# First-group tables in two pairs: into-state tables turned unscaled, scales put into the out-of-state tables

## The chip, the cores and the metric

The kernel runs on one core of a Trainium2 chip. The metric is the device time of one execution in microseconds (us); lower is better. The engines spoken of are TensorE (PE in the profile; PEld is its weight load), Vector (DVE), ScalarE (ACT), GpSimd (POOL) and Sync (SP, which here only issues DMAs). A name with q (SPq) is an engine's queue of DMA issues.

## The reference

For 64 batches, 64 heads and 1024 positions, x passes through a state-space convolution and then a gated low-rank feed-forward layer, and is added to the result:

```python
# per head h: 64 complex states n
dtA = (-exp(log_A_real) + 1j*A_imag) * exp(log_dt)[:, None]
Cs  = (C[...,0] + 1j*C[...,1]) * (exp(dtA) - 1.0) / A
K   = 2.0 * einsum('hn,hnl->hl', Cs, exp(dtA * l)).real      # length 1024
u_m = x * mask                                               # l < length[b]
y   = (causal convolution of u_m with K + u_m * D) * mask
# tokens are rows of y of 1024 features
scores = y @ Wr.T                        # 64 experts
gates  = softmax of the 16 largest scores
h   = einsum('nd,krd->nkr', y, A)        # 64 experts of rank 16
out = x + 2.0 * einsum('nkr,kdr->nd', h * gates, B)
```

All is float32.

## The kernel before

The 1024 positions of a head are cut into 8 chunks of 128. Within a chunk the convolution is a 128x128 Toeplitz matrix; between chunks it goes through the 64 complex states. So each head needs four kinds of table, made from its parameters: the *into-state* table (turned, so that it can be the stationary operand of the matmul that takes a chunk into the states; tile `bt`), the *out-of-state* table (tile `w`), the factor by which a state goes on over one chunk (tile `turn`), and the Toeplitz matrix (tile `toep`). The tables are values of exp(dtA l) at l of the constant row `lv`: magnitude exp(re l) from ScalarE (`mag`), sine and 1 - 2 sin^2 of half the angle from ScalarE's Sin (`sn`, `sh`), the angle reduced to one turn by Vector. Before the change the into-state table carries the scale of C: `alpha`, `nbeta`, `nalpha` are columns with one value for each state of a head, computed by a chain of small Vector operations from the parameters (`exp_parts`, `real_part`, `angle`, `products`).

Heads go in 8 groups of 8 (`HG`); a group has 4 pairs of heads (`GP`), and one tile holds a pair, 64 states of each head on 128 partitions. Group g runs as `conv(g)`: `into_states` (the `pu` matmuls, L742, copied out by ScalarE, L747) for each pair, `recur` on Vector over the 7 chunks (L786), `inside` (Toeplitz products into `pc` banks, L828 and L836), `across` (states out through `w`, L851), `evict` (Vector, times the length mask, L862). Then come gates and the feed-forward products (`first`, L687, tile `h`), which use a seven-product scheme for 2x2 blocks. The factors of A for that scheme are sums of its quarters: the first eight are formed on TensorE by identity matmuls (`factors_by_identity`, L211, seen as `sum`, copied out by ScalarE L216 and L220); two more sums are accumulating DMAs that GpSimd issues after the copy `landed` (L224), which waits for the last Toeplitz load.

The first group is special: nothing runs before it. Its tables come from `tables(0)`, stepped by hand. For each pair, Vector scales `w` into `b` (L497, L503), TensorE transposes it (`turned_table`, L440, tile `pb`), ScalarE copies it to `bt` (L442). For each two pairs, `kernels` multiplies the scaled table by the matrix `heads` (L328, `pk`), which adds the states of each head to the row of K; ScalarE copies it (`ks`, L331 to L333), Vector adds D, Sync stores it to `krows` in HBM (L372), and three loads (L356) read it back shifted by one element for each partition, which gives `toep`.

What order things run in:

- While `first_order` is open, Vector runs in the order in which the code names its operations; while `first_copies` is open, so does ScalarE.
- On TensorE, GpSimd and the queues a planner picks the order by estimated readiness and program order, except where `keep_in_program_order` pins an instruction behind the one before it on its engine, and `issue_after` behind a named one.
- `together` takes one step of each of several generators in turn, `some(it, n)` takes n steps.
- `ps_k` has 2 PSUM buffers, for `pb`, `pk` and the first group's `pu`. `ps_f` has 4, for `sum`, for `pc` of pairs 1 and 3 of the first group, and for `h`. `ps_c` has 2, for `pc` of pairs 0 and 2.

Of the kernel before, what the change touches and what calls it, by code (L numbers as in the profile page):

```python
# [44 lines left out]
P = 128  # L45
NB = 64
# [61 lines left out]
def body(ctx: ExitStack, tc, x, xo, lens, par, dvec, dgrp, at, bm, wt, cst, out):  # L108
# [36 lines left out]
    lens_sb = prep.tile([P, NB], I32, tag="lens", name="lens_sb")  # L145

# [14 lines left out]
    def load_x(h):  # L161
        t = xp.tile([P, 2, NBLK * NB], F32, tag="x", name=f"x_{h}")
        marks["x"] = nc.sync.dma_start(t, x[h : h + 2].rearrange("h p c -> p h c"))
        x_tiles[h] = t
# [8 lines left out]
    def quarters(wpool, w, name, queue, fine=False):  # L173
# [16 lines left out]
        for n, i in ((0, 0), (1, 0), (0, 2), (1, 2), (2, 0), (2, 2), (3, 0), (3, 2))[2 * fine :]:  # L190
            load(n, i)
# [51 lines left out]

    wa_quarters = quarters(wp, at, "wa", nc.sync, True)
    load_x(0)
    nc.sync.dma_start(lens_sb, lens.partition_broadcast(P))
    load_x(2)
    load_x(4)
    load_x(6)
# [19 lines left out]
    scales = {}  # L269

    def tables(g):
# [43 lines left out]
        if g == 0:  # L315
            turn, toep = others()
            tabs[g] = (w, bt, turn, toep)
        h0 = g * HG
        if g == 0:
            all_rows = tabp.tile([2, GP, P], F32, tag="mag", name=f"ks_{g}")  # L320

        def kernels(bbs, i):


            n = i + 2 * len(bbs)
            pk = ps_k.tile([2, n - i, P], F32, tag="pk", name=f"pk_{g}_{i}")
            for m, bb in enumerate(bbs):
                nc.tensor.matmul(pk[:, 2 * m : 2 * m + 2, :], lhsT=heads, rhs=bb[:, :, 0, :],  # L328
                                 start=True, stop=True)
            ks = all_rows[:, i:n, :]  # L330
            nc.scalar.copy(ks, pk)  # L331
            nc.scalar.copy(ks[0:1, :, :HP], pk[0:1, :, HP:])
            nc.scalar.copy(ks[0:1, :, HP:], pk[0:1, :, :HP])  # L333
            return ks, i, n
# [14 lines left out]
        def load_toeplitz(i, n):  # L349


            row = krows[h0 + 2 * i : h0 + 2 * i + 1, :]
            heads_of = toep[:, 2 * i : 2 * n, :].rearrange("p (i a) c -> p a i c", a=2)

            def load(o, count, start):
                nc.sync.dma_start(  # L356
                    o, bass.AP(row.tensor, row.offset + start, [[1, count], [2 * KROW, n - i], [1, P]]))

# [85 lines left out]
        for i in range(GP if g < DIRECT else 0):  # L444
# [14 lines left out]
            if g:  # L459
                if i % 2:  # L460
                    yield
# [1050 lines left out]
```

## Time and profile before

| | us |
|---|---|
| median of 3 runs (lowest, highest) | 941.73 (941.72, 941.85) |
| the profiled execution's own time | 941.79 |
| its span, first to last instruction | 940.0 |
| TensorE busy | 929.5 |
| Vector busy | 741.0 |
| GpSimd busy | 337.0 |
| ScalarE busy | 164.1 |

The page of the profile shows busy times and shares of the span, the span in 40 slices, the chain of work that ended last (followed back from the last instruction to what released each step), and groups of instructions by line. A line of a timeline has the start, the duration, the engine, the line, the operation, output and inputs, how many instructions were merged, and in brackets the idle time before and what ended it. A line of the chain has start, duration and what. Times are in us from the start of the span; a mean of one instruction is in ns. A float32 matmul is two passes, and so two instructions; a transpose is one. Buffer numbers are left out of names: `was` and `waa` are quarters and sums of A.

### The profile page before, as it was taken

To read this page: it belongs to the slowest core of one execution; us is meant where nothing else is said; L and a number is where in the kernel's file an instruction comes from. 1 tells how busy PE (TensorE), PEld (TensorE's weight loads), DVE (VectorE), ACT (ScalarE), POOL (GpSimd) and SP (SyncE) were. 2 spreads that over 40 slices of the span, in tenths; PEclk is the share of its full clock that TensorE was granted. 3 is DMA by queue.
4 is the path that set the end of the run, shared out by engine and by line. 5 is a ranking of instruction groups with operands and counts; after the bars stand their busy time and mean duration, and the time that the engine had idled before them with its cause. 6 is when DMAs were issued, how large, how long until landed. Compare 5 with 4: busy or idle time off the path is not lost.

```text
span 940.0 us, 14255 instructions
## 1 busy us (share of the span) xinstructions
PE 929.5 (99%) x5384; PEld 743.2 (79%) x5384; DVE 741.0 (79%) x1725; ACT 164.1 (17%) x314; POOL 337.0 (36%) x284
## 2 busy tenths in 40 slices
PE   7999999999999999999999999999999999999998
PEld 2576768688588588588588788888888888888887
DVE  8899798797996995995892497879856866785674
ACT  5343233411411411510300000000000000000000
POOL 0113213052052052052052032356746555764555
PEclk9999999999999999999999999999999999999999
DMA  8635335347454444444242463754672574358332
GB/s 291 186 87 168 107 110 156 108 126 189 125 144 154 124 138 159 125 128 169 90 131 101 152 246 124 255 203 140 212 275 79 191 270 155 110 205 307 95 123 101
DMA packets 72298, 149.47 MB, mean 159 GB/s; under 512 B 10054, under 2 KB 21030, under 8 KB 72230
## 3 DMA queue, kind: packets, MB, share of 16 engines
q1 hardware_dynamic: 52546, 99.65, 32.1%
q0 software_dynamic: 16864, 47.22, 16.0%
q10 hardware_dynamic: 2820, 1.70, 0.6%
q8 instruction: 42, 0.69, 0.3%
q14 instruction: 26, 0.21, 0.1%
HBM read 100.13 MB, written 47.33 MB: 157 GB/s over the span
## 4 chain that ended last, share of the span: by engine, by line
PE 93%; DVE 6%; issue 0%; DMA 0%; ACT 0%; DVEq 0%
PE h L687 39%; PE s L1272 35%; PE pu L742 5%; PE pc L851 4%; PE psh L947 3%; PE pc L828 3%; PE pc L836 1%; DVE bt L492 1%; DVE hg L492 1%; DVE f L492 1%; DVE f L503 0%; PE psc L959 0%; PE pb L440 0%; PE last L1272 0%; DMA par_sb<-in_par 0%
## 5 line engine op out<-in xcount | busy, mean ns | idle before, releaser
L786 DVE SCALAR_TENSOR_TENSOR s<-s,turn 128x64 f32<-128x64 f32 (+1 forms) x432 | 122.8, 330 | 2.8 <-ACT s L747 2.3
L687 PE MATMUL h<-y,waa 128*128 128x256 f32 x512 | 116.7, 380 | 0.0
L687 PE MATMUL h<-y,was 128*128 128x256 f32 x512 | 116.2, 379 | 0.0
L687 PE MATMUL h<-ty,was 128*128 128x256 f32 x512 | 116.0, 379 | 0.0
L687 PEld LDWEIGHTS h<-y,waa 128*128 128x128 f32 x512 | 96.3, 190 | 15.0 <-issue 1.9
L687 PEld LDWEIGHTS h<-ty,was 128*128 128x128 f32 x512 | 97.1, 190 | 13.9 <-issue 0.8
L687 PEld LDWEIGHTS h<-y,was 128*128 128x128 f32 x512 | 96.8, 190 | 13.7 <-DVE b L503 0.4
L1034 POOL TENSOR_TENSOR hg<-h_p,gx 128x512 f32<-128x512 f32 x16 | 35.6, 2223 | 141.6 <-DVE h_p L503 107.1
L1007 POOL DMA_DIRECT2D gx<-gt_dram x56 | 33.9, 618 | 145.1 <-DMA gt_dram<-gt 145.1
L1286 ACT COPY p<-s 128x512 f32<-128x512 f32 x28 | 16.4, 585 | 312.4 <-PE s L1272 312.4
L1034 POOL TENSOR_TENSOR hg<-h_u,gx 128x512 f32<-128x512 f32 x32 | 45.1, 1409 | 63.8 <-DVE h_u L492 36.6
L1131 POOL TENSOR_TENSOR o<-o,acc_a 128x512 f32<-128x512 f32 x32 | 47.6, 1506 | 41.4 <-ACT acc_a L1149 32.5
L687 PE MATMUL h<-ty,waa 128*128 128x256 f32 x256 | 58.4, 381 | 0.0
L687 PEld LDWEIGHTS h<-ty,waa 128*128 128x128 f32 x256 | 48.2, 190 | 8.3 <-DVE rsn L492 0.8
L742 PE MATMUL pu<-x,bt 128*64 128x448 f32 x256 | 53.0, 546 | 0.4
L862 DVE TENSOR_TENSOR y<-pc,mask 128x512 f32<-128x512 f32 x64 | 40.2, 680 | 16.4 <-PE pc L851 16.4
L1131 POOL TENSOR_TENSOR o<-o,b_room 128x512 f32<-128x512 f32 x32 | 49.1, 1555 | 9.8 <-DVE b_room L492 9.8
L492 DVE TENSOR_TENSOR o<-o,s 128x512 f32<-128x512 f32 x50 | 34.1, 681 | 23.0 <-PE s L1272 17.9
L1037 POOL DMA_DIRECT2D hg_dram<-hg x32 | 25.6, 800 | 67.4 <-DVE hg L492 46.6
L1131 POOL TENSOR_TENSOR o<-o,u 128x512 f32<-128x512 f32 x36 | 45.3, 1282 | 10.0 <-DVE u L492 9.7
L492 DVE TENSOR_TENSOR hg<-hg 128x512 f32<-128x512 f32 x64 | 42.4, 682 | 4.7 <-POOL hg L1034 4.3
L1272 PE MATMUL s<-qy,wbs 128*128 128x256 f32 x192 | 44.1, 379 | 0.0
(275 smaller groups left out, 1678.8 us busy)
## 6 DMA issues: line engine op xcount, KB each, us to landing
x<-in_x SPq DMA_DIRECT2D x32, 512.0 KB
hg_dram<-hg POOLq DMA_DIRECT2D x16, 1024.0 KB, 6.0
o<-in_xo SPq DMA_DIRECT2D x64, 256.0 KB
out<-o SPq DMA_DIRECT2D x63, 256.0 KB
gx<-gt_dram POOLq DMA_DIRECT2D x56, 256.0 KB, 4.8
qy<-hg_dram SPq DMA_DIRECT2D x28, 512.0 KB
r<-hg_dram SPq DMA_DIRECT2D x26, 512.0 KB
hg_dram<-hg POOLq DMA_DIRECT2D x16, 768.0 KB, 4.5
```

Of the source, the lines that this page charges most:

```text
L492: V.tensor_tensor(out=o, in0=a, in1=b, op=o_)
L687: nc.tensor.matmul(bank[:, ii, :], lhsT=fac[n - 1][:, k, (j + ii) * P : (j + ii + 1) * P], rhs=rf[n - 1][:, k, :], start=(first and ii == ...
L742: nc.tensor.matmul(pu[hh * NS : (hh + 1) * NS, :], lhsT=bt[:, i, (1 - c) * P + hh * NS : (1 - c) * P + (hh + 1) * NS], rhs=xt[:, hh, : NCH ...
L786: return V.scalar_tensor_tensor(out=o, in0=a, scalar=scalar, in1=b, op0=op0, op1=op1)
L828: nc.tensor.matmul(pcs[hh][half_of(e, 1), chunks(e)], lhsT=toep[:, 2 * i + hh, HP:], rhs=xt[:, hh, chunks(e)], start=True, stop=False, ski ...
L851: m = nc.tensor.matmul(pcs[hh][half_of(e, late), into], lhsT=w[o : o + NS, c, i, seg : seg + HP], rhs=s[o : o + NS, c, of].rearrange("p k ...
L862: marks["y"] = V.tensor_tensor(out=y[:, :, i // 2, 2 * (i % 2) + hh, :], in0=pcs[hh].rearrange("p (k b) -> p k b", b=NB), in1=mask, op=ALU ...
L947: nc.tensor.matmul(phalf[o : o + NE, :], lhsT=wt_sb[:, d, :], rhs=yf[:, d, :], start=(d < 2), stop=(d >= NBLK - 2),)
L1007: i = queue.dma_start(gx[:, ii, :], gt_dram[g, c * n : (c + 1) * n, :].unsqueeze(1).to_broadcast([n, RANK, TOK]),)
L1034: G.tensor_tensor(out=o, in0=a, in1=b, op=op)
L1131: tc.keep_in_program_order(G.tensor_tensor(out=o, in0=a, in1=b, op=op_))
L1272: nc.tensor.matmul(bank[:, ii, :], lhsT=left_[i - 1][:, k, ii * P : (ii + 1) * P], rhs=right_[i - 1][:, k, :], start=(first and ii == rows ...
```

## The change

For the first group only:

- `half_of_tables(n)` forms magnitude, sine and cosine for two pairs at a time, into `u` (unscaled, imaginary part in `u[:, 1]`).
- The into-state tables are `u`, unscaled, turned by four matmuls against the identity (`turned_first`); the chunk states so lack the scale of C.
- The scale is put into the out-of-state table `w` instead (`scaled`): a multiplication by one column, then another and an addition. For pairs 0 and 1, component 0 is done by Vector; all others by a ScalarE multiplication, a GpSimd multiplication (into the room of `mag`) and a GpSimd addition.
- The rows of K come from component 0 of the scaled `w` (`kernels_of`); D is added by GpSimd instead of Vector.
- `turn` is copied from `u`; its signs change places.
- Of the eight steps of sums on TensorE, one comes before the first half tables' steps and two after it, one after the first two turned tables, and four after the last `pu` matmul of pair 3.
- States of pairs 2 and 3 are made before `recur(0, 1)` is named instead of after it.
- The mask is made by eight Vector operations in turn with the first `exp_parts`, instead of one later; the lengths it needs are loaded on ScalarE's queue behind the constants, instead of on Sync's queue behind the first tile of x.
- Sync loads the group's four tiles of x before the last two pieces of A instead of after them, pinned in that order.

```diff
     cst_sb = ids.tile([P, NW + P + 2 + NBLK + 1], F32, tag="cst", name="cst_sb")
     nc.scalar.dma_start(cst_sb, cst)
     lens_sb = prep.tile([P, NB], I32, tag="lens", name="lens_sb")
+    nc.scalar.dma_start(lens_sb, lens.partition_broadcast(P))
...
+        for n, i in rest[:-2]:
+            load(n, i)
+        if between is not None:
+            between()
+        for n, i in rest[-2:]:
             load(n, i)
...
-    wa_quarters = quarters(wp, at, "wa", nc.sync, True)
-    load_x(0)
-    nc.sync.dma_start(lens_sb, lens.partition_broadcast(P))
-    load_x(2)
-    load_x(4)
-    load_x(6)
+    wa_quarters = quarters(wp, at, "wa", nc.sync, True, lambda: [load_x(h) for h in range(0, HG, 2)])
...
+    def half_of_tables(n):
...
+        u = first_tables[n] = prep.tile([P, 2, 2, NW], F32, tag=f"u{n}", name=f"u_0_{n}")
+        for m in range(2):
+            nc.scalar.activation(mag[:, m, :], lv, AF.Exp, scale=dt_re[:, i + m : i + m + 1])
+        yield
+        tt(f, tu_hi[:, i : i + 2].unsqueeze(2).to_broadcast(wide), lv.unsqueeze(1).to_broadcast(wide), ALU.mult)
+        yield
+        ts(k, f, MAGIC, ALU.add, MAGIC, ALU.subtract)
+        yield
+        tt(f, f, k, ALU.subtract)
+        yield
+        for m in range(2):
+            stt(f[:, m, :], lv, tu_lo[:, i + m : i + m + 1], ALU.mult, f[:, m, :], ALU.add)
+        yield
+        ts(f, f, HALF_IN, ALU.min, -HALF_IN, ALU.max)
+        nc.scalar.activation(k, f, AF.Sin, scale=math.pi)
+        nc.scalar.activation(sn, f, AF.Sin, scale=2.0 * math.pi)
+        yield
+        nc.scalar.activation(k, k, AF.Square)
+        nc.scalar.activation(k, k, AF.Copy, scale=-2.0, bias=1.0)
+        yield
+        tt(u[:, 1], mag, sn, ALU.mult)
+        tt(u[:, 0], mag, k, ALU.mult)
+        yield
...
+    def masks():
+        lens_f = prep.tile([P, NB], F32, tag="lensf", name="lens_f")
+        for _ in range(4):
+            yield
+        V.tensor_copy(lens_f, lens_sb)
+        for k in range(NBLK):
+            yield
+            ts(mask[:, k, :], lens_f, feat[:, k : k + 1], ALU.is_gt)
+
+    together(exp_parts(log_both, "e", 2 * NP, parts), masks())
...
-    steps0 = tables(0)
-    next(steps0)
+    half_tables = [half_of_tables(n) for n in range(2)]
+    for t in half_tables:
+        next(t)
+    next(half_tables[0])
     for _ in some(sums, 1):
         pass
-    together(some(steps0, 5), real_part(), angle())
+    together(some(half_tables[0], 5), real_part(), angle())
+    for _ in some(sums, 2):
+        pass
+    next(half_tables[0])
...
-    together(products(), some(steps0, 2))
-    scales.update(alpha=alpha, nbeta=nbeta, nalpha=nalpha)
-
-    for _ in some(sums, 7):
-        pass
-    first_copies.close()
...
+        def turned_first(i):
+            pb = ps_k.tile([P, 2 * P], F32, tag="pk", name=f"pb_0_{i}")
+            for c in range(2):
+                for seg in range(2):
+                    nc.tensor.matmul(
+                        pb[seg * HP : (seg + 1) * HP, (1 - c) * P : (2 - c) * P],
+                        lhsT=first_tables[i // 2][:, c, i % 2, seg * SEG : seg * SEG + HP], rhs=ident,
+                        start=(c == 0), stop=(c == 1), skip_group_check=True)
+            nc.scalar.copy(bt[:, i, :], pb)
+
+        def scaled(i, c, scale, add):
+            u = first_tables[i // 2]
+            by, also = ((alpha, nbeta), (nbeta, nalpha))[c]
+            scale(w[:, c, i, :], u[:, 0, i % 2, :], by[:, i : i + 1])
+            if add is V:
+                stt(w[:, c, i, :], u[:, 1, i % 2, :], also[:, i : i + 1], ALU.mult, w[:, c, i, :], ALU.add)
+            else:
+                t = first_tables["mag", i // 2][:, i % 2, :]
+                add.tensor_scalar(out=t, in0=u[:, 1, i % 2, :], scalar1=also[:, i : i + 1], scalar2=None,
+                                  op0=ALU.mult)
+                add.tensor_tensor(out=w[:, c, i, :], in0=w[:, c, i, :], in1=t, op=ALU.add)
...
+        def kernels_of(i):
+            pk = ps_k.tile([2, 2, P], F32, tag="pk", name=f"pk_0_{i}")
+            nc.tensor.matmul(pk, lhsT=heads, rhs=...)   # w[:, 0, i : i + 2]
+            ks = all_rows[:, i : i + 2, :]
+            nc.scalar.copy(ks, pk)
...
+            G.tensor_tensor(out=ks[:, :, 0], in0=ks[:, :, 0], in1=d_sb[:, i : i + 2], op=ALU.add)
+            nc.sync.dma_start(
+                krows[2 * i : 2 * i + 4, P - 1 :].rearrange("(i a) l -> a i l", a=2), ks)
+            load_toeplitz(toep, 0, i, i + 2)
...
         if g == 0:
-            step(1)
+            all_rows = tabp.tile([2, GP, P], F32, tag="mag", name="ks_0")
+            turned_first(0)
+            turned_first(1)
+            for _ in some(sums, 1):
+                pass
+            together(products(), some(half_tables[1], 5))
+            scales.update(alpha=alpha, nbeta=nbeta, nalpha=nalpha)
             into_states(0, 0, bt, states, more)
+            next(half_tables[1])
             into_states(0, 1, bt, states, more)
-            step(3)
-            masks()
+            for i in range(2):
+                scaled(i, 0, by_vector, V)
+            kernels_of(0)
+            next(half_tables[1])
+            for n in range(2):
+                turns_of(n)
             first_order.close()
-            step(1)
+            for i in range(2):
+                scaled(i, 1, by_scalar, G)
+            turned_first(2)
+            turned_first(3)
+            into_states(0, 2, bt, states, more)
+            into_states(0, 3, bt, states, more)
+            for i in range(2, GP):
+                scaled(i, 0, by_scalar, G)
+            kernels_of(2)
+            for i in range(2, GP):
+                scaled(i, 1, by_scalar, G)
+            with tc.issue_after(marks["pu"].ins):
+                for _ in some(sums, 4):
+                    pass
+            first_copies.close()
             behind_landing(toep[0:1, HG - 1, 0:1])
...
         recur(0, 1)
         if g == 0:
-            into_states(0, 2, bt, states, more)
-            into_states(0, 3, bt, states, more)
             first_two = inside(0, 1)
```

## Prediction

> **What bounds the kernel now.** I read the page's shares first, then the chain of waits, then the timelines of the five queues from 0 to 52 us, which is all that the change touches.
>
> ```profile
> PE 929.5 (99%) x5384; PEld 743.2 (79%) x5384; DVE 741.0 (79%) x1725; ACT 164.1 (17%) x314; POOL 337.0 (36%) x284
> ```
>
> TensorE is busy 929.5 of 940.0 us. Only its late start (4.14 us, then 1.43 us waiting for a piece of A) and waits in the first group are there to be won; whatever delay is left when the first group ends is carried to the end at full size. From the chain:
>
> ```profile
> 18.92 0.12 DVE p_nbeta L497
> 19.04 0.09 DVE p_nalpha L497
> 19.14 0.39 DVE b L497 x2
> ...
> 20.76 0.59 PE pb L440 x2
> 21.35 0.52 PE pk L328 x2
> 21.88 3.50 PE pu L742 x16
> ...
> 33.22 3.03 PE pc L851 x64
> 36.25 2.35 PE pc L828 x15
> ```
>
> Until 20.7 us the end hangs on Vector (parameters, tables, scaling of each table); after that on TensorE, which goes from the states (pu) to the Toeplitz products (pc L828, pairs 0-1 at 30.25, pairs 2-3 at 36.25). TensorE's timeline shows what it does while Vector works:
>
> ```profile
> 9.48 1.91 PE L211 MATMUL sum<-was,cst_sb 128*128 128x512 f32 x2
> 11.19 1.91 PE L211 MATMUL sum<-waa,cst_sb 128*128 128x512 f32 x2
> 12.90 1.96 PE L211 MATMUL sum<-was,cst_sb 128*128 128x512 f32 x4
> 14.70 5.31 PE L211 MATMUL sum<-waa,cst_sb 128*128 128x512 f32 x12
> 19.85 0.59 PE L440 MATMUL pb<-cst_sb,b 128*128 128x128 f32 x2
> ```
>
> The identity sums fill it until 20.0, just when Vector's first table (19.96) arrives. So half of what an earlier table wins is lost at once: those sums still have to run, only later. How much waiting hides inside "busy"? By cadences of steady rows (h 16 passes in 3.46 us, so 0.216 a pass of 256 columns and 0.433 of 512; half-array passes of pc 0.108; pu 32 in 6.16, 0.1925; quarter-array pc 0.054 and 0.047), the work from 14.70 to 46.4, the end of the first group, is 12 sum passes 5.2 + pb 0.9 + pk 0.9 + pu 6.2 + L828 3.5 + L836 1.7 + L851 6.0 + h 3.5 = 27.8 us, of 31.7. About 4 us are waits.
>
> **The change, step by step.** The clock is that of the profiled execution: 941.79 us, span 940.0 with 1.79 around it; the median 941.73 is 0.06 lower.
>
> Mask. Nine small Vector operations go into the gaps of the first exponential, where each dependent step of 64 elements takes 0.23-0.25 us though it needs about 0.1 to issue. Cost 0 (all in gaps) to 0.9 (nine at 0.1), I take 0.2; 0.9 us at 23.05-23.97 goes away. It makes Vector wait for the lengths, whose load moves from Sync (issued 9.54) to ScalarE's queue behind the constants: issue about 1.2. The constants took 0.75 to 4.04, so by them it lands at 4.5, and Vector asks at 4.55. Behind it is the whole parameter chain. Bounds: 0, and 3 us (the second piece of A, issued 1.66, was waited for until 7.62). I take 0.2, by the constants, its own queue. The zero rows' DMA on ScalarE's queue moves back by one issue (0.4), under the idle time before the 4.04 table load: nothing.
>
> Half tables. The first pair costs Vector half of (0.61+0.34+0.61+1.06+0.34): 1.5 instead of 2.96. The interleaved parameter steps stay 3.35. So u of pairs 0-1 is ready at 9.18+0.4+1.55+3.35+0.66 = 15.15, against 19.96 for the first scaled table.
>
> Turning. A table was two transposes (0.108 each); it is now eight passes of 128 columns on half the array, 0.055 each by pu and pc, 0.45: +0.22 a table, +0.9 us on TensorE in all (bounds 0 and 2.6, if the halves don't overlap). TensorE then runs sum 4 of the first kind (1.75) and reaches pu at 17.5 (sum first) to 18.0 (tables first), against 21.82.
>
> ScalarE's order is written by hand, so it now paces TensorE, whose states share two PSUM buffers. From 18.0, with rows 0.53 (448 and 512 wide), 0.38 (bt), 0.8 (three ks copies), 0.3 (128x131): sum copy 18.55, two sines 19.2, states of pair 0 20.2, Square and Copy 20.9, states of pair 1 21.9, ks 22.75 (pk at 21.4), two scalings 23.3, two bt copies 24.0, then four states at 0.8 behind TensorE: 27.4. TensorE ends pu at 26.8, with waits of about 1.9. Then come the four late sums (3.46) and pk (0.43), which used to be over at 20: 30.8, not 30.25. Product order on TensorE is the planner's; a sum first or a pk first moves this by 0.5.
>
> A new wait: pairs 1 and 3 of the Toeplitz products use the banks of those sums. ScalarE copies them only behind ks of pairs 2-3 and two scalings, at 31.8 and 32.3; pair 1 is asked for at 31.7. Cost 0.2-0.6. TensorE would turn to pairs 2-3 at about 37.1 instead of 36.25: +0.8.
>
> The Toeplitz matrices of pairs 2-3 are what I think ends last. Before:
>
> ```profile
> 27.88 0.25 SPq L372 DMA_DIRECT2D krows<-ks  x1
> 29.02 1.87 SPq L356 DMA_DIRECT2D toep<-krows  x3
> ```
>
> ```profile
> 34.04 0.35 POOL L224 COPY landed<-toep 1x1 f32<-1x1 f32 x1 [33.10 <-DMA toep<-krows]
> ```
>
> From the row store to landing are 6.16 us, with 2.2 to spare before 36.25. Now the rows wait for scaled tables: ScalarE's two scalings stand behind the states (27.75, 28.0), then GpSimd multiplies and adds, three operations in line, then pk 0.5, ks 0.8, GpSimd's add 0.35, the store. No row has GpSimd on 128x131.
>
> ```profile
> L1034 POOL TENSOR_TENSOR hg<-h_p,gx 128x512 f32<-128x512 f32 x16 | 35.6, 2223 | 141.6 <-DVE h_p L503 107.1
> L1131 POOL TENSOR_TENSOR o<-o,u 128x512 f32<-128x512 f32 x36 | 45.3, 1282 | 10.0 <-DVE u L492 9.7
> ```
>
> By width these give 0.33 and 0.57; the single-element copy above took 0.35. Bounds 0.33 and 1.28 (no saving from width); I take 0.5, nearest to the contended row since Vector runs without pause here. Tables 29.3, store 31.1, landing 37.3. If pk stands behind the sums in TensorE's queue (30.4), the landing is 38.4; at 1.28 an operation 39.7. I take 38.3 for it: +2.05 against 36.25.
>
> The GPSIMD Engine Reference of the Trainium skill (Engine selection, and the side-by-side accounting) speaks against this move: elementwise work belongs on VectorE, about 2.6 cycles an element at 1.2 GHz here. By it alone an operation would be an estimated 0.28 us, the landing about 0.7 earlier, and the sum +1.4.
>
> What is freed. Vector loses sixteen scalings (3.7 us at 19.05-22.72) and gains four, so its recurrence starts at 22 instead of 24.36. That brings little: it ended at 32.8 before, TensorE took it up at 33.22. Sync issues x before the last two pieces of A, which first products at 39.55 need: nothing. GpSimd's sums of A start 3-4 us later, at about 38, landing near 58 for the last, needed at 69.3: nothing. Everything behind is TensorE without waits, so the delay stays.
>
> The clock is a second place where the sums matter: a pass of 512 columns took 0.855 us before 12.9 and 0.433-0.445 after, while the granted-clock column reads 1.00. I expect no return to the slow rate, since the longest gap that I find is 0.4 us, against 1.43 in the row at 7.62 that came before the change of pace.
>
> TensorE: Matmul & The Clock Gate (What's actually happening) puts that gap's limit at about 3.4 us of idleness; a wait for the lengths of that length is the only place where no row here tells.
>
> Sum: 941.73 + 2.05 = 943.8 us.
>
> **Rivals.**
>
> Toeplitz rows in time. If GpSimd takes 0.35 an operation and the planner puts pk between the sums, the landing is 36.8 and the bank wait is what is left: +0.8, 942.5 (+0.1 to +1.6). For it: it needs no favour beyond the low row.
>
> Faster. The waits, not the work, are removed: the count falls only from its 31.7 us to 28.7 (27.8 + 0.9) if nothing waits, 3.0 us at most. If the sum stands before the turned tables and the four late sums lie exactly in the rows' flight, half to three quarters is kept: 1.5 to 2.3, 939.4 to 940.2, say 939.6. It decides if store 2 leaves before about 29.5 us and the banks are free at 31. Against it: ScalarE's queue alone reaches 27.4 by its rows. That any gain above 3.0 us would have to come from rows that the change doesn't touch is why I give it little.
>
> Lengths late. If the lengths land like the second piece of A, Vector stands up to 3 us, and everything hangs on it: +3 to +5 with the Toeplitz wait, 946. It decides from a landing past 5 us.
>
> **How the numbers follow.** 0.2% of the time, 1.9 us, is about what a measurement of this kernel can tell from no change. Toeplitz rows late 0.40 (0.34 beyond 943.6, 0.06 within), in time 0.28 (within), faster 0.18 (0.12 beyond, 0.06 within), lengths late 0.14 (beyond): faster 0.12, same 0.40, slower 0.48. The likeliest alone is 943.0 to 945.0. The range 940.3 to 946.6 leaves out the better part of the gain's tail and the worst of the late lengths, 0.2 together.
>
> **What would show it.** Right: pu begins near 18 us; ScalarE has no gap from 18 to 24; the first-group products begin near 31; the second landing copy on GpSimd stands at 37-39, and TensorE's pass to pairs 2-3 waits for a DMA. Wrong: a store of rows 2 before 30 us, TensorE's pairs 2-3 before 36, a Vector wait for the lengths above 0.5 us, a sum pass of 0.85 us after 15 us, or a difference that arises after the first group, where I expect none.

## The result, and the profile after

The changed kernel takes 945.37 us, the median of 6 executions (944.41 to 945.87), against 941.79 (941.66 to 941.88) for the kernel before on the same chip: a ratio of 1.0037, 95% interval 1.0024 to 1.005. It is 3.6 us slower. The profiled execution took 944.9 us with a span of 943.1, against 941.79 and 940.0.

The share line of the changed kernel's page:

```profile
PE 928.4 (98%) x5408; PEld 743.4 (79%) x5408; DVE 737.2 (78%) x1728; ACT 165.5 (18%) x324; POOL 344.6 (37%) x298
```

Vector gave up 3.8 us, as the change meant it to, and GpSimd took 7.6. TensorE's busy time fell by 1.1 while the span grew by 3.1: TensorE has not more to do, it waits more. Where it waits is in the chain that ended last (start, duration, what):

```profile
1.18 4.70 DMA lens_sb<-in_lens
...
5.91 0.04 DVE lens_f L559
...
20.07 0.43 ACT s L754
...
20.54 1.75 PE pu L749 x8
...
28.45 0.31 ACT w L907
...
28.89 0.54 POOL w L904
...
30.73 0.59 PE pk L915 x2
```

Before, the chain went over Vector to 20.7 us and then stayed on TensorE. Now it starts with the load of the lengths, which was in flight for 4.70 us, goes over Vector again, and after the states of pairs 2 and 3 it leaves TensorE once more, for a ScalarE scaling and three GpSimd operations in line. TensorE's timeline over the same stretch (start, duration, line, operation, tiles, shape, count, and in brackets the idle time before):

```profile
5.54 2.04 PE L219 MATMUL sum<-was,cst_sb 128*128 128x512 f32 x2 [5.54 <-DMA was<-in_at]
7.38 1.84 PE L219 MATMUL sum<-waa,cst_sb 128*128 128x512 f32 x2
9.06 1.02 PE L219 MATMUL sum<-was,cst_sb 128*128 128x512 f32 x2
...
16.70 1.10 PE L887 MATMUL pb<-cst_sb,u 128*64 128x128 f32 x16 [1.98 <-DVE u L498]
17.83 1.72 PE L749 MATMUL pu<-x,bt 128*64 128x448 f32 x8
20.54 1.72 PE L749 MATMUL pu<-x,bt 128*64 128x448 f32 x8 [0.98 <-ACT s L754]
...
30.73 0.59 PE L915 MATMUL pk<-w,cst_sb 128*2 128x256 f32 x2 [0.94 <-POOL w L904]
31.25 1.98 PE L219 MATMUL sum<-waa,cst_sb 128*128 128x512 f32 x4
33.16 2.00 PE L838 MATMUL pc<-x,toep 128*64 128x256 f32 x16
```

The same places before:

```profile
21.82 3.53 PE L742 MATMUL pu<-x,bt 128*64 128x448 f32 x16
...
30.25 1.95 PE L828 MATMUL pc<-x,toep 128*64 128x256 f32 x16
...
36.18 2.42 PE L828 MATMUL pc<-x,toep 128*64 128x256 f32 x16
```

After the first sum, three waits of 1.98, 0.98 and 0.94 us stand in the timeline of after; before, the largest from the first table on was 0.33. The first states begin at 17.83 instead of 21.82, four microseconds earlier; the first products begin at 33.16 instead of 30.25, 2.9 later. Pairs 2 and 3 follow at 39.14 instead of 36.18, and the score products `psh` of groups 0 and 1 at 53.30 and 122.98 instead of 50.50 and 120.19: 2.8 at both. Of the 3.1 us of the span, the other 0.3 comes behind the last matmul, which ends 2.8 us later too (939.33 against 936.52); from there to the end of the span are 3.79 us instead of 3.48. That closing stretch is 3.93 in e5 and 3.49 in e6, so it does not follow the time of the kernel.

Vector at the place where the chain enters it:

```profile
5.91 0.20 DVE L559 CAST lens_f<-lens_sb 128x64 f32<-128x64 int32 x1 [1.31 <-DMA lens_sb<-in_lens]
...
9.00 0.19 DVE L498 TENSOR_TENSOR p_dtre<-p_are,p_both 128x32 f32<-128x32 f32 x1
```

The last of these steps before:

```profile
7.21 0.19 DVE L492 TENSOR_TENSOR p_dtre<-p_are,p_both 128x32 f32<-128x32 f32 x1
```

Vector is idle for 1.31 us, and then each step of the exponential takes 0.30 us, since a mask operation stands between each two, against 0.25 before. `p_dtre`, which heads everything else, starts at 9.00 instead of 7.21: 1.31 of waiting and 0.48 of interleaving.

Sync's queue, first before, then after:

```profile
2.13 0.47 SPq L181 DMA_DIRECT2D was<-in_at  x1
3.22 0.33 SPq L181 DMA_DIRECT2D waa<-in_at  x1
```

```profile
3.36 0.33 SPq L184 DMA_DIRECT2D was<-in_at  x1
5.90 0.33 SPq L184 DMA_DIRECT2D waa<-in_at  x1
```

The early load also holds up others: Sync's third and fourth issues, which are pieces of A, are at 3.36 and 5.90 us, where they were at 2.13 and 3.22, and the first sum waits until 5.54 for its piece instead of 4.14. (They are late in every profile with the early load, and back at 2.12 and 2.99 in e2, which undoes it.)

GpSimd and Sync at the end of the chain, and GpSimd at the landing of the Toeplitz matrices:

```profile
28.89 0.53 POOL L904 TENSOR_TENSOR w<-w,mag 128x131 f32<-128x131 f32 x1 [3.82 <-ACT w L907]
29.52 0.66 POOL L902 TENSOR_SCALAR mag<-u,p_nalpha 128x131 f32<-128x131 f32 x1
...
39.37 0.18 POOL L232 COPY landed<-toep 1x1 f32<-1x1 f32 x1 [5.89 <-DMA toep<-krows]
```

```profile
32.51 0.25 SPq L924 DMA_DIRECT2D krows<-ks  x1
```

The rows of pairs 2 and 3 are stored at 32.51 us (27.88 before), and the matrices land at 39.37, against 34.04. TensorE reaches for them at 39.14: they cost it 0.25 us (the pass takes 2.25, against 2.00 in runs where they are in time). Before, the same pass took 2.42, for waits of another kind: its weight loads waited 0.7 us for Vector's eviction of the pairs ahead.

### The profile page after: what moved, and what is told of

It is laid out like the page before. It is cut to its first block, busy times and chain, and to the rows that moved or that the text cites. A ratio compares the mean times of both kernels' runs of the same rounds, so it can differ in the third digit from the quotient of the medians.

```text
span 943.1 us, 14333 instructions
## 1 busy us (share of the span) xinstructions
PE 928.4 (98%) x5408; PEld 743.4 (79%) x5408; DVE 737.2 (78%) x1728; ACT 165.5 (18%) x324; POOL 344.6 (37%) x298
## 4 chain that ended last, share of the span: by engine, by line
PE 92%; DVE 6%; DMA 0%; issue 0%; ACT 0%; POOL 0%; ACTq 0%; DVEq 0%; POOLq 0%
PE h L694 39%; PE s L1357 35%; PE pu L749 5%; PE pc L861 4%; PE psh L1032 3%; PE pc L838 3%; PE pc L846 1%; DVE bt L498 1%; DVE hg L498 1%; DVE f L498 1%; DMA lens_sb<-in_lens 0%; DVE f L509 0%; PE psc L1044 0%; PE last L1357 0%; PE pb L462 0%
## 5 line engine op out<-in xcount | busy, mean ns | idle before, releaser
L796 DVE SCALAR_TENSOR_TENSOR s<-s,turn 128x64 f32<-128x64 f32 (+1 forms) x432 | 120.8, 326 | 1.4 <-ACT s L754 0.9
```

What stands on the lines that cost most here:

```text
L796: return V.scalar_tensor_tensor(out=o, in0=a, scalar=scalar, in1=b, op0=op0, op1=op1)
```

## The experiments

Three explanations compete: the lengths and the mask at the head of Vector's chain; the late scalings, by ScalarE behind the states and then by GpSimd, with the rows of K behind them; and the first sums, that is the loads of A and TensorE's change of pace. A fourth came up on the way. In the table, "profiled" is the profiled execution, and the starts are in us in it.

| kernel | median (lowest to highest), runs | profiled | first pc | pairs 2-3 | psh of group 1 |
|---|---|---|---|---|---|
| before | 941.79 (941.66 to 941.88), 6 | 941.79 | 30.25 | 36.18 | 120.19 |
| after | 945.37 (944.41 to 945.87), 6 | 944.90 | 33.16 | 39.14 | 122.98 |
| e3_before_mask_early | 943.44 (943.11 to 943.95), 11 | 943.37 | 31.82 | 37.74 | 121.8 |
| e1_mask_late | 943.82 (942.68 to 944.91), 11 | 944.87 | 33.01 | 38.99 | 123.0 |
| e2_lens_undone | 945.54 (942.76 to 946.05), 5 | 942.76 | 31.14 | 37.12 | 120.7 |
| e4_lens_first | 944.78 (944.44 to 945.43), 5 | 944.44 | 32.95 | 38.93 | 122.5 |
| e8_change_scale_first | 943.44 (942.99 to 944.84), 11 | 944.45 | 31.44 | 37.42 | 122.5 |
| e5_scale_first | 942.98 (941.90 to 944.38), 11 | 941.90 | 30.26 | 36.24 | 119.83 |
| e6_vector_scale | 942.48 (941.84 to 943.29), 11 | 942.75 | 31.27 | 37.24 | 120.8 |
| e7_loads_undone | 946.72 (945.82 to 948.12), 5 | 947.08 | 33.95 | 39.93 | 125.0 |
| e9_warm | 945.55 (945.30 to 946.01), 5 | 945.30 | 33.82 | 39.80 | 123.4 |
| e10_sums5 | 945.53 (944.77 to 946.07), 5 | 944.77 | 33.18 | 39.16 | 122.8 |
| e11_second_look | 944.40, 1 | 944.40 | 31.31 | 37.29 | 122.3 |
| e12_late_factors | 942.29 (941.70 to 942.95), 11 | 942.55 | 30.92 | 36.90 | 120.48 |

The kernel before, run beside them, stayed between 941.63 and 941.90 every time. The changed kernels do not repeat so well: their executions differ by 0.7 to 3.3 us. So a single profile and a median can differ by 1 us or more, and both are given. The result, e1 to e4, e5 to e8 and e9 to e12 are separate series, the last three on three chips. The medians of the kernel before agree between them within 0.1 us; of the changed kernels only e2 ran in two series (e11).

### The mask and the lengths

**e3_before_mask_early.** The kernel before, with the mask part alone:

```diff
+    nc.scalar.dma_start(lens_sb, lens.partition_broadcast(P))      # behind the constants
...
-    nc.sync.dma_start(lens_sb, lens.partition_broadcast(P))
...
-    together(exp_parts(log_both, "e", 2 * NP, parts))
+    together(exp_parts(log_both, "e", 2 * NP, parts), masks())     # nine small operations
...
-            masks()                                                # the one operation of before
```

> The kernel before with the mask part of the change alone (lengths behind the constants on ScalarE's queue, eight mask operations in turn with the first exponential). Theory A: Vector is what the end hangs on until 20.7 us, so its delay of 1.3 to 1.8 us at dt_re passes to the end, less the 0.9 us of the mask that goes away later, which lay beside TensorE's work: 943.1 to 943.6 from 941.8. Rival B gives the mask part nothing to do with the loss: 941.8 within 0.4.

It takes 943.44, a ratio of 1.0019 (1.001 to 1.0028): 1.7 us for this part alone, as Theory A expected. Vector and TensorE in its timeline:

```profile
5.70 0.20 DVE L553 CAST lens_f<-lens_sb 128x64 f32<-128x64 int32 x1 [1.13 <-DMA lens_sb<-in_lens]
```

```profile
21.41 0.59 PE L440 MATMUL pb<-cst_sb,b 128*128 128x128 f32 x2 [0.74 <-DVE b L503]
```

Nearly the same wait (1.13 against 1.31), and the first table 1.56 us later (19.85 before). The delay is found again at full size in the products (31.82 against 30.25) and in the total. In the kernel before, Vector's chain sets the end until 20 us, so nothing hides it.

**e1_mask_late.** The changed kernel with the mask formed by one Vector operation after the scalings, the lengths still on ScalarE's queue:

```diff
-    together(exp_parts(log_both, "e", 2 * NP, parts), masks())
+    together(exp_parts(log_both, "e", 2 * NP, parts))
...
                 turns_of(n)
+            masks()
             first_order.close()
```

> The changed kernel with the mask formed in one Vector operation after the turn columns, as in the kernel before; the lengths still loaded on ScalarE's queue behind the constants. Theory A (the lengths): in the changed kernel's profile Vector stands 1.31 us for the lengths at 5.91 and each of the next steps takes 0.30 instead of 0.25 us, so dt_re comes at 9.00 instead of 7.21; everything behind hangs on it, so 1.8 us come back: 943.1 to 943.6, and the runs, which spread over 1.5 us, agree within 0.3. Rival B (the late scales): ScalarE's order and GpSimd's three operations before the second pk set the end of the first group whatever Vector does earlier; the time stays above 944.7 and the wait of TensorE for GpSimd grows.

The median falls by 1.55 to 943.82 (ratio 1.0022, 1.0013 to 1.0031), 0.2 above Theory A's range, and the executions spread by 2.2 us instead of 0.3. Its profiled execution, at 944.87, is one of the longest and shows what is left: `p_dtre` is back at 7.3, but Sync's third and fourth issues still stand at 3.44 and 5.80, the sums wait for pieces of A, and the first `pu` waits 1.10 us for x. Vector no longer waits for the early load, but TensorE's own inputs are still late, and its first products (33.01) come only 0.15 us earlier than in the profile of after. So the gain stands in the median and not in this profile.

**e2_lens_undone.** e1 with the load of the lengths back on Sync's queue:

```diff
-    nc.scalar.dma_start(lens_sb, lens.partition_broadcast(P))
...
+        load_x(0)                                                   # on Sync, pinned in this order
+        tc.keep_in_program_order(nc.sync.dma_start(lens_sb, lens.partition_broadcast(P)))
+        for h in range(2, HG, 2):
+            load_x(h)
```

> As the one before, and the lengths' load put back on Sync's queue between the first and second tile of x: the whole mask part of the change undone, the rest kept. Theory A with a share for the transfer (the first piece of A was waited for until 5.54 us instead of 4.14, the lengths' load being the only new traffic ahead of it): the first sum starts near 4.1, but TensorE waits for the tables anyway, so the time is that of the kernel with the late mask alone within 0.3 us, 943.1 to 943.6. If the lengths' traffic also held up the parameters or constants: another 0.5 us or more lower. Rival B: above 944.7.

In its profile the head is repaired: the first sum at 3.97, the turned tables at 15.53 without a wait, products at 31.14, 942.76 us. But its other four executions took 945.12 to 946.05, and the median, 945.54, is not below that of the changed kernel: it is above 944.7, as Rival B said, although the whole mask part is undone. (The same step where the scalings already stand first, from e8 to e5 on one chip, wins 0.46.) This kernel and e1 therefore cannot tell what the load alone is worth, and why four of five lay so high is explained only in part, below (e11).

**e4_lens_first.** The changed kernel with the lengths loaded ahead of the constants:

```diff
+    nc.scalar.dma_start(lens_sb, lens.partition_broadcast(P))
     nc.scalar.dma_start(cst_sb, cst)
-    nc.scalar.dma_start(lens_sb, lens.partition_broadcast(P))
```

> The changed kernel with the lengths' load ahead of the constants on ScalarE's queue; the mask is still formed early. Theory A, if the lengths were late because they stood behind 135 KB of constants: they land about 1.2 us earlier, Vector's wait goes, only the 0.05 us a step is left: 943.9 to 944.3. If instead the load itself is slow (128 reads of the same 256 bytes): issue to landing stays near 4.7 us, 0.4 us are won at most: 944.9 to 945.4. Rival B: 945.4 within 0.4.

944.78, within the range of the changed kernel, and 0.1 below the range expected of a load that is itself slow. Vector no longer waits for the lengths; instead the constants arrive at 5.90, the parameters at 4.4, and `pb` waits 1.69 us for `u`. In both places tried this broadcast among the first loads makes something late; the order only chooses what.

### The scalings behind the states

**e8_change_scale_first.** The changed kernel, with ScalarE's (and so GpSimd's) scalings for pairs 2 and 3 named ahead of their states:

```diff
             turned_first(3)
+            for i in range(2, GP):
+                scaled(i, 0, by_scalar, G)
             into_states(0, 2, bt, states, more)
             into_states(0, 3, bt, states, more)
-            for i in range(2, GP):
-                scaled(i, 0, by_scalar, G)
```

> The changed kernel itself with only ScalarE's two scalings moved ahead of the states of pairs 2 and 3. Theory A (the lengths' wait is the main loss) with C: 0.9 of TensorE's wait for GpSimd and the rest of the landing's lateness are won, 944.0 to 944.6 from 945.4, and the runs agree within 0.8 us since only the lengths' landing still varies. If the moved scalings delay the states of pairs 2 and 3 as much as they save: 945.0 to 945.5.

The median falls by 1.9 to 943.44 (ratio 1.0021, 1.0013 to 1.0029), more than the 0.8 to 1.4 expected. TensorE's timeline:

```profile
27.29 0.59 PE L915 MATMUL pk<-w,cst_sb 128*2 128x256 f32 x2
27.81 3.70 PE L219 MATMUL sum<-waa,cst_sb 128*128 128x512 f32 x8
31.44 2.00 PE L838 MATMUL pc<-x,toep 128*64 128x256 f32 x16
```

`pk` comes straight behind the states, without the 0.94 us wait, and the four sums run behind it in the time of the rows' flight; the Toeplitz matrices land at 34.74, 2.7 us before they are wanted. The first products are 1.72 us earlier than in the profile of after. Of that, 0.54 is there already when the states begin (17.29 against 17.83), since the lengths landed sooner in this execution (`p_dtre` at 8.44 against 9.00); 1.18 comes behind it, and 0.25 more at pairs 2 and 3. So the profile gives the scalings 1.4 of the 1.9. The early tables are the same in both kernels and don't set this loss; the place of the scalings in ScalarE's hand-written order does.

**e5_scale_first** is the same move on e2, and **e6_vector_scale** gives the four operations of pairs 2 and 3 to Vector instead, as the change itself does for pairs 0 and 1:

```diff
             for n in range(2):
                 turns_of(n)
+            for i in range(2, GP):
+                scaled(i, 0, by_vector, V)
...
-            for i in range(2, GP):
-                scaled(i, 0, by_scalar, G)
```

> The kernel with the mask part undone, and ScalarE's two scalings of component 0 of pairs 2 and 3 named before the states of those pairs instead of after them, so that GpSimd can finish the tables earlier and the second pk stands ahead of the four late sums. Its runs without the move went from 942.76 to 946.05, in the profiled one the last Toeplitz load landed just as TensorE turned to pairs 2 and 3 (36.9 against 37.12). Theory C (that landing, now without reserve, varies from run to run): the row store leaves 2 us earlier, TensorE's wait of 0.84 for GpSimd goes, the spread falls below 0.5 us, 941.9 to 942.5. Theory D (the early loads vary: the tiles of x now go ahead of the last pieces of A and are used 4 us earlier): median and spread stay, 945.5 and 3 us.

> As the one before, but component 0 of pairs 2 and 3 is scaled by Vector (two operations each, 1.2 us in all, after the turn columns) instead of by ScalarE and GpSimd: the GpSimd chain of three operations ahead of the second pk is gone and ScalarE has two operations less. Theory C: as before, 941.9 to 942.5 with a spread below 0.5; Vector has 2 us of reserve before it evicts pairs 0 and 1. If GpSimd was what made the landing late, and not the order, this one is the faster of the two by 0.3. Theory D: 945.5 with a spread of 3 us.

942.98 (ratio 1.0011, 1.0002 to 1.002) and 942.48 (1.0008, 0.9999 to 1.0017). In both, `pk` does not wait and the matrices are in time (33.37 and 34.55). Theory C's range is missed by 0.5 and just met, but the spreads, 2.5 and 1.45 us, are not below 0.5, so neither theory holds as it was put. With mask, lengths and scalings undone, what is left of the change, half tables and unscaled turning above all, costs 0.7 us in the median of e6, with an interval that reaches 1, and has executions as short as the kernel before. It does not gain: in e5's profile the products begin at 30.26, against 30.25. The first table is turned 4.5 us earlier (15.38 against 19.85); 3.6 of it goes to the four sums that now run behind the states, and the rest to the turning, which takes longer, and to waits for ScalarE's copies (0.58 and 0.19).

### The loads of x

**e7_loads_undone.** e2 with the x tiles, and the lengths between them, behind the last two pieces of A again:

```diff
-        if between is not None:
-            between()
         for n, i in rest[-2:]:
             load(n, i)
+        if between is not None:
+            between()
```

> The kernel with the mask part undone and also the order of the loads: the four tiles of x and the lengths behind the last two pieces of A, as in the kernel before. The tiles land some 2.6 us later, the first near 16 us, where it is wanted at 16.7. Theory D: if the order of the loads makes the spread, it falls below 0.5 us; the time is 942.8 to 943.8, depending on whether the last tiles make TensorE wait. Theory C: the spread stays near 3 us, the median near 945.5.

946.72, 1.2 above e2 (ratio to before 1.0054, 1.0041 to 1.0066) and above both ranges expected; the spread stays, at 2.3 us. The states wait 1.87 us for x. In the kernel before, the states asked for x at 21.8; now they do so at 17, and its new place in the queue is needed.

### TensorE's change of pace

A pair of sum passes takes 2.04 us early on and 1.02 later, and the granted clock reads 1.00 all the time. The change of pace comes at 9.06 us in the profile of after, at 11.0 in e5's, at 12.9 before, at 13.1 in e6's. It moves between two profiles of one kernel as well: 11.6 in e2, 10.5 in e11. Eight passes that run slow cost 0.42 us each, and only a kernel whose first tables wait for the sums feels it.

**e9_warm.** e6, with small multiplications of a zero tile before the first sum and in the wait for its second piece, to bring the fast rate forward (the two products of the first sum are pinned in order with them):

```diff
+        warm(8)                                  # 64x64 weights, 127 columns, two passes each
         for k in range(KH):
             add(banks[k], a21[:, k, :], first=True)
+            if k == 0:
+                warm(10)
             add(banks[k], a22[:, k, :])
```

> The kernel with the mask part undone and Vector scaling pairs 2 and 3 (942.48, 941.84 to 943.29), and TensorE kept busy from the start: eight small matmuls of a zero tile before the first sum and ten between its two inputs. In the profiles of this series TensorE's passes of 512 columns go from 0.855 to 0.433 us at times between 9.1 and 13.1 us after the start, and the time follows: 941.9 where the change of pace came at 11.0, 942.75 where it came at 13.1. Theory E (what still varies is the moment of that change, which the kernel before hides since Vector is what it waits for until 20.7 us): the sums run fast throughout, the tables of pairs 0 and 1 are turned when Vector has them, near 15.0, and the time is 941.3 to 941.9 with a spread below 0.4 us. Theory D (the early loads vary): median 942.5 and a spread above 1 us, as without the extra work.

```profile
0.98 3.64 PE L229 MATMUL warm<-zero 64*64 64x127 f32 x16 [0.98 <-POOL zero L564]
4.55 2.07 PE L220 MATMUL sum<-was,cst_sb 128*128 128x512 f32 x2
6.56 4.49 PE L229 MATMUL warm<-zero 64*64 64x127 f32 x20
10.98 2.07 PE L220 MATMUL sum<-waa,cst_sb 128*128 128x512 f32 x2
```

TensorE is busy without a break from 0.98 us, and the sums still run slow until 15.3: the small passes did not bring the fast rate, and they delayed the sums. `pb` comes at 19.30 instead of e6's 16.75, and the time is 3.1 above e6's median and above both ranges expected. As a way to gain it failed; it does show that the end follows the end of the sums, since 2.55 us at `pb` are 2.55 at the first products (33.82 against 31.27).

TensorE: Matmul & The Clock Gate of the Trainium skill (What's actually happening) lets about 3.4 us of sustained work release the gate, in windows that do not start with the kernel. By the rows here it took 3.5 us of unbroken sums in after (5.54 to 9.06) and 5.1 of the same unbroken sums in e3 (5.52 to 10.6); before, some 9 us of sums with a gap of 1.4; and in e9 more than 14 us of work that was mostly small passes on zeros, 4.4 us of sums behind the last of them. What counts as work no run here tells.

**e10_sums5.** e9 with one late sum moved ahead of the turned tables:

```diff
-    for _ in some(sums, 2):
+    for _ in some(sums, 4):
...
-            for _ in some(sums, 1):
-                pass
...
-                for _ in some(sums, 4):
+                for _ in some(sums, 3):
```

> As the one before, and one of the four late sums formed ahead of the turned tables, in the time in which TensorE then waits for Vector. Theory E: 0.45 us less work stands behind the states, so 0.3 to 0.45 below the kernel before it in this series, 940.9 to 941.6, spread below 0.4. If ScalarE's extra copy ahead of the turned tables delays them (0.53 us): no gain, 941.3 to 942.0.

945.53, the same as e9 (945.55), and above both ranges expected. In the medians a sum moved from behind the tables to before them gains nothing. The two profiles cannot price the move: the change of pace comes at 14.4 in e10 and at 15.3 in e9, `pb` is 0.3 later and the products 0.6 earlier.

### What varies after the first group

**e11_second_look.** e2 once more, unchanged.

> The kernel with the whole mask part undone once more, for a profile of one of its slow executions: of five, one took 942.76 (the profiled one) and four 945.1 to 946.1. Theory E: the profile shows the change of pace after 13 us and everything behind it 1.3 to 1.7 us later, 944 or more. Theory D: it shows TensorE waiting for a tile of x, 1 us or more. Theory C: it shows TensorE waiting at pairs 2 and 3 for the Toeplitz loads.

944.40, 1.6 us above e2's profile: the score products of group 0 are 0.4 us later (51.45 against 51.02), and from there to those of group 1 1.2 us more are lost. Of the 0.4, 0.26 is the wait that Theory C named, for the Toeplitz loads of pairs 2 and 3 (that pass takes 2.26 instead of 2.00); the signs of E and D are not there, since the change of pace comes at 10.5 and no tile of x is waited for. The 1.2 are in none of the three theories. The place is in TensorE's timeline:

```profile
108.18 3.72 PE L696 MATMUL h<-y,was 128*128 128x256 f32 x16 [0.92 <-DVE h_p L514]
```

and the reason in GpSimd's, first e2, then e11:

```profile
75.52 1.28 POOL L1122 TENSOR_TENSOR hg<-h_p,gx 128x512 f32<-128x512 f32 x1 [2.55 <-DVE hg L1129]
```

```profile
77.55 1.28 POOL L1122 TENSOR_TENSOR hg<-h_p,gx 128x512 f32<-128x512 f32 x1 [4.14 <-issue]
```

The eight gate tiles `gx` took a median of 5.9 us from issue to landing in e2 and 6.7 in e11, and GpSimd's first gate product starts 0.3 us behind the landing of the fourth in both (75.22 and 77.25), so 2.0 later. In the changed kernels Vector's sums of these products stand early in its order (79 to 84 us, against 87 before), so Vector waits for GpSimd: 4.4 us in e2, 6.0 in e11. The recurrence behind them is late by as much, and in the second case TensorE waits for Vector some 27 us later. All profiles with this order of Vector agree: with landings of 5.2 to 6.0 Vector waits 4.2 to 4.8 and TensorE not at all (after, e1, e2, e4, e5, e6, e9, e10); with 6.7 to 7.0 Vector waits 6.0 to 6.3 and TensorE 0.9 to 1.2 (e7, e8, e11). The kernel before, with the later sums, has landings of 6.4 and TensorE does not wait.

**e12_late_factors.** e5, with these sums kept behind the first multiplications of the recurrence, as they stand in the kernel before:

```diff
             def sums():
+                with tc.issue_after(marks["rec"].ins):    # a multiplication of the last recurrence named
+                    form()
+
+            def form():
                 tt(t1, b11, b12, ALU.subtract)
```

> The kernel with the mask and lengths part undone and the w scalings of pairs 2 and 3 ahead of the states (e5), and one thing more: Vector's four hg sums of group 0 are kept behind the first multiplications of the next recurrence, where the kernel before has them (it starts them near 87 us, the changed kernels near 79 to 82). Theory A: with these sums early, Vector waits 4.2 to 4.8 us for GpSimd's gate products, and where the eight gx tiles land at a median over 6.5 us after their issue it waits 6.0 to 6.3 us and TensorE then loses 0.9 to 1.2 us near 108 us; this is the later loss that e7, e8 and the second profile of e2 show, and it makes much of the spread of the changed kernels. Then the new kernel shows no wait of TensorE for h_p near 108 us whatever gx takes, Vector's wait for hg falls under 1 us, the gap from psh_0 to psh_1 is 69.7 us, the median falls from e5's 942.98 to 941.8 to 942.3 and the spread of runs from 2.5 to about 1 us. Theory B: the spread of e5 comes from the first 20 us alone (the moment of TensorE's change of pace and the loads). Then the median stays at 942.6 to 943.2 with a spread of 2 us or more. If the order is worth more than the late landing (the sums early also delay the recurrence) the time could fall to 941.3 or below, under the kernel before.

```profile
75.61 2.95 DVE L798 SCALAR_TENSOR_TENSOR s<-s,turn 128x128 f32<-128x128 f32 x3 [0.94 <-ACT s L756]
...
87.39 0.68 DVE L503 TENSOR_TENSOR hg<-hg 128x512 f32<-128x512 f32 x1
```

Vector starts the recurrence at 75.61 and does not wait for `hg` at all. The gate tiles took 6.6 us, as in the disturbed profiles, and TensorE does not wait; from `psh` of group 0 to that of group 1 are 69.68 us, as before. The median is 942.29 (ratio 1.0004, 0.9995 to 1.0013), 0.7 below e5, and the executions span 1.25 us instead of 2.5, all as Theory A expected. The single profile agrees with the later wait being removed; the lower spread is what it would do, but the two kernels were timed on different chips. No version beats the kernel before in the median; this one is not distinguishable from it.

## Why the prediction was right or wrong

Slower came out, and the time lies in the range, 1.6 us above the number and 0.4 above the 943.0 to 945.0 called likeliest. The sign was right, but that the number comes near is in part luck: the sum had pairs 2 and 3 start 2.05 late, 0.8 of it because TensorE is late itself (37.1) and 1.2 as the wait for the landing (38.3). Measured, TensorE was 2.96 late itself and the wait was 0.25. By its condition (a landing past 5 us, measured 5.88) and its range (3 to 5 us) the rival Lengths late, given 0.14, fits the result better than the sum, and of the signs of being wrong one came in the changed kernel: Vector waits 1.31 us for the lengths, not below 0.5.

- **The lengths.** This is the step that failed most. I took 0.2 for the wait and 0.2 for the nine operations, because the constants on the same queue had landed in 3.3 us. The broadcast took 4.70 and landed at 5.88; the terms are 1.31 and 0.48 at `p_dtre`. The rival Lengths late named this mechanism and its sign (past 5 us) rightly, but gave it the delay of the second piece of A, 3 us; alone, on the kernel before, the mask part is 1.7 us (e3).
- **The start of the states.** 17.83, within the 17.5 to 18.0 predicted, but for another reason: the tables were 1.5 us late, while the sums before them were early by the change of pace at 9.06. Two errors cancelled, and hid what the lengths cost at this point.
- **ScalarE paces TensorE.** It does, with the 0.98 wait for `s`; but it has a gap of 0.63 at 19.34, for Vector's `f`, which the late lengths pushed back (e2 and e6, without the early load, have no gap there, and a wait of 0.25 for `s`). I had expected no gap. States end at 27.87, not 26.8.
- **Products at 30.8.** They came at 33.16. Of the 2.36, 1.07 is the states, 0.94 TensorE's wait for GpSimd's `w` ahead of `pk`, which I had not placed in TensorE's queue at all, and the rest 0.35 longer sums and `pk`.
- **The Toeplitz rows.** The store at 32.51 (31.1), the landing at 39.37 (37.3 or 38.4, and the window of 37 to 39 given as a sign): its start was 1.4 late, and the flight took 6.86 us where I took the 6.16 of before (5.6 to 7.0 in the runs). But TensorE was itself at 39.14 by then, so the wait for the landing, 1.2 in the sum, was 0.25. The late scalings cost their 1.4 to 1.9 us (e8) mostly one step earlier, at `pk`, behind which half the sums and the products stand. The cause named was right, the place was not.
- **GpSimd's operations.** Additions took 0.41 to 0.55, multiplications by a column 0.62 to 0.73; 0.5 was taken for each. The GPSIMD Engine Reference of the Trainium skill (Engine selection; Elementwise — side-by-side cycle accounting) advises VectorE for such work, and by its cycles I had estimated 0.28; the measurement decides, and it is 1.5 to 2.6 times that. e6, which follows the advice, has a median 0.5 below e5's, less than the spread of either.
- **The bank wait** of 0.2 to 0.6 did not appear: no `pc` of the first group waits for a copy of a sum.
- **The order of x.** Costed at nothing; it is needed, and without it the states wait 1.87 us for x and the median is 1.2 higher (e7).
- **Nothing after the first group.** In the profile of after this holds: 2.8 us at both score products. It does not hold in general: the new order of Vector puts a wait at 79 us, which in some executions of such kernels costs TensorE 0.9 to 1.2 us more (e7, e8, e11).

Of the 3.6 us, the mask part is worth 1.7 on the kernel before (e3), where nothing else changes. In the changed kernel its worth is not settled: 1.55 by the median of e1, nothing by that of e2, 0.46 from e8 to e5. The late scalings are 1.9 by the median of e8, 1.4 by its profile and 2.6 from e2 to e5. Both undone, and the lengths' load with them, leave 0.7 (e6) or, with the order of Vector's sums undone too, 0.5 (e12), which the runs do not tell from nothing. That the two parts together make the loss is shown so; how it divides between them is not, since the parts act on one chain and the medians carry the spread of the executions.

Open: why four executions of e2 lay at 945 to 946 (e11, which is not as slow, accounts for 1.6 of the 2.8 us above its first profile), and why the gate tiles land sooner in some executions than in others.

## What to carry to other kernels

A load that is moved to the front is not free because its new queue is idle: price it by a row of the same shape, and look at whose loads it delays. When a stage is made earlier, ask what it ran beside: here the sums that filled TensorE's wait had to be run all the same, and an earlier table won nothing that the runs can tell. Where a hand-written order gives work to an engine that paces another, put what starts a long chain (scaling, row, store, load) ahead of what only has to be done by then.

## What the runs showed of the hardware

- The lengths, 256 bytes broadcast to 128 partitions, took 4.70 us at the start of the program. With that load there, the next issues of another queue moved from 2.13 and 3.22 to 3.36 and 5.90, and back to 2.12 and 2.99 without it (e2).
- TensorE's passes run at half pace until 9 to 13 us, at a moment that differs from kernel to kernel and between two profiles of one kernel (11.6 in e2, 10.5 in e11), while the granted clock reads 1.00; 36 small passes on zeros did not bring it forward (15.3 in e9).
- On GpSimd a 128x131 multiplication by a column took 0.62 to 0.73 us in after, an addition of two tiles of that size 0.41 to 0.55; over all profiles the medians are 0.64 and 0.49, and a single addition took up to 1.08 (e5).
- The kernel before, whose end hangs on Vector for its first 20 us, repeats within 0.3 us; the changed kernels, whose TensorE takes up each table and load as it comes, spread by 0.7 to 3.3 us. The profiles show the early loads, the change of pace and the landing of the gate tiles vary; which makes how much of the spread is not shown.
